# The last stage of a graph kernel: chunks of six buckets summed in PSUM, products on GpSimd, scaled nodes in PSUM

## The chip, the cores and the metric

The kernel runs on one core of one Trainium2 chip. The core has five engines with a queue of instructions each: TensorE (PE in the profile, with its weight loads as PEld), VectorE (DVE), ScalarE (ACT), GpSimd (POOL) and SyncE (SP), which starts transfers here. Each engine works through its queue in order and waits at semaphores for what the others have to deliver. SBUF holds tiles of 128 partitions; PSUM is the memory that TensorE writes its sums to, in 8 banks. The metric is the time of one execution on the device in microseconds, the median of the runs.

## The reference

A graph has N = 6250 nodes with F = 128 features and E = 100,000 edges. The reference runs two graph layers, each followed by a residual and a layer norm. The last stage belongs to the second, cut here to what it computes (`x` is the output of the first layer norm, `edge_attr` has 128 features an edge):

```python
xt = logmap0(x, C)                       # x scaled by one number a node
xs = xt[src]
adj_att = sigmoid(concat([xs, xt[dst], edge_attr]) @ att_w.T + att_b)
agg_add  = segment_sum(xs * adj_att, src, N)
mean_src = segment_sum(edge_attr, src, N) / cnt_src      # cnt = max(edges of the node, 1)
mean_dst = segment_sum(edge_attr, dst, N) / cnt_dst
support_t = xt + agg_add + mean_src + mean_dst
x = layernorm(x + proj(expmap0(support_t, C), C))
```

Since `xs` is summed by its own node, `agg_add` is the node's row times its sum of attentions. `expmap0`, `proj` and the last layer norm need, for each node, the sums of the means, of their squares and of their products with `x`, and then scale whole rows by numbers of the node.

## The kernel before

The kernel sorts edges into 49 *buckets* of 128 source nodes each. Rows of 132 numbers (128 edge features, a one for the count, the attention, and the node's place in its bucket) are scattered by GpSimd's indirect transfers (`scatter`, L812) into tables in memory. The tables of later edges are `lates`; the one of the last edges has 256 rows a bucket, that is two blocks of 128. A bucket is summed by matmuls: `bucket_load` (L1556) fetches its rows into one of four slots of `acc[:, 2]`, `bucket_hot` (L1573) has DVE compare the places with the columns, which makes a one-hot matrix (`oh`, two buffers), and `bucket_mm` (L1587) multiplies it with the rows, so that PSUM holds the features' sums, the count and the attention's sum of 128 nodes (S = 130 columns). `bucket_add` (L1601) adds that to `sums_` in SBUF. In the profile each float32 matmul stands as two passes.

All that runs in a long loop over groups of edges (L1699 to 1718), in an order written out by hand. The *last stage* begins when the last group is scattered: it sums the last table and finishes the nodes. Its order isn't written by hand; a scheduler places its instructions on the engines from their dependencies.

- `chunk(b0)` (L1742) works on CB = 7 buckets. It loads, sums and adds them in two units of four and three. It takes the counts' reciprocals `rc`, and for each bucket DVE adds the mean to `sup` (`mean_dst` so far) and takes its sum `ts` (L1752), and ACT takes the squares' sum `tt` (L1756). DVE multiplies `sup` with the nodes `x1` (L1758) and reduces the products to `tx` (L1759).
- `finish(b0, b1)` (L1761) makes, from `ts`, `tt`, `tx` and the attentions' factor `f`, the three numbers `h`, `m` and `fac` of each node. It is a chain of some 26 short DVE instructions with three ACT functions between (square root L1779, hyperbolic tangent L1781, square root L1796), each change of which loads a table. Then, bucket by bucket, ACT scales the nodes in place (L1805) and DVE adds the scaled `sup` (L1806); SP stores chunks (L1810), and the last part of a bucket by itself (L1818).

Four chunks are followed by `finish(0, 28)`, three by `finish(28, 49)`. PSUM holds the columns' numbers (`beside`, L673), three buffers `bp` of two buckets' sums, and a small check `pq` (L1726).

Of the kernel before, what the change touches and what calls it, by code (L numbers as in the profile page):

```python
# [16 lines left out]
P = 128  # L17
# [585 lines left out]
def window_path(ctx, tc, bad, x, src, dst, edge_attr, edge_weight, Wm1, bm1, Wm2, bm2, Wm3, bm3,  # L603
# [98 lines left out]
    def column(b, name):  # L702
        t = const.tile([F, 1], F32, name=name)
        later(t, b[:, None])
        return t
# [842 lines left out]
        return todo  # L1548
    todo = plan()

    with tc.tile_pool(name="bwork", bufs=2, reuse_waits="tile") as bwork, \
            tc.tile_pool(name="bp", bufs=3, reuse_waits="tile", space=PSUM) as bp:

        n_load = 0

        def bucket_load(us):  # L1556

            nonlocal n_load
            at = n_load % 4 * BR * RW
            n_load += 1  # L1560
            bts = []
            for i, h0, nh in us:
                t, cap = AT[i]
                c = cap // P
                bt = acc[:, 2, at:at + nh * c * RW].rearrange("p (h c f) -> p h c f", h=nh, f=RW)
                at += nh * c * RW
                nc.sync.dma_start(
                    bt.rearrange("p h c f -> p h (c f)"),
                    t[h0 * cap:(h0 + nh) * cap].rearrange("(h p c) f -> p h (c f)", p=P, c=c))
                bts.append(bt)  # L1570
            return bts
# [15 lines left out]
        def bucket_mm(us, bts, ohs):  # L1587
            pbs = []
            for (i, h0, nh), bt, oh in zip(us, bts, ohs):
                c = bt.shape[2]  # L1590
                for a in range(0, nh, 2):
                    pb = bp.tile([P, 2, S], F32, name="pb")
                    n = min(2, nh - a)
                    for h in range(n):
                        for j in range(c):
                            nc.tensor.matmul(pb[:, h], lhsT=oh[:, a + h, j], rhs=bt[:, a + h, j, :S],  # L1596
                                             start=j == 0 and h == 0, stop=j == c - 1 and h == n - 1)
                    pbs.append((i, h0 + a, n, pb))
            return pbs

        def bucket_add(pbs):  # L1601
            for i, h0, n, pb in pbs:
                t = sums_[:, h0:h0 + n]
                if i == 0:
                    nc.scalar.copy(t, pb[:, :n])
                else:
                    nc.vector.tensor_add(t, t, pb[:, :n])

        with tc.tile_pool(name="awork", bufs=2, reuse_waits="tile") as awork, \
                tc.tile_pool(name="ap1", bufs=3, reuse_waits="tile", space=PSUM) as ap1, \  # L1610
                tc.tile_pool(name="ap2", bufs=1, reuse_waits="tile", space=PSUM) as ap2, \
                tc.manual_schedule():
# [110 lines left out]
        with tc.tile_pool(name="fwork", bufs=2, reuse_waits="tile") as fwork, \  # L1723
                tc.tile_pool(name="fp", bufs=1, reuse_waits="tile", space=PSUM) as fp:

            pq = fp.tile([1, P], F32, name="pq")  # L1726
            nc.tensor.matmul(pq, lhsT=badc, rhs=ident, start=True, stop=True)
            nc.vector.tensor_reduce(bad, pq, AX.X, OP.max)

            CB = 7
            assert NB % CB == 0
            last = len(GENS)

            def wide(name):
                return fwork.tile([P, NB], F32, name=name, bufs=1)
            ts, tt, tx, q1, f1 = (wide(n) for n in ("ts", "tt", "tx", "q1", "f1"))
            nc.vector.tensor_mul(q1, mv[:, :, 1], rstd)
            nc.vector.scalar_tensor_tensor(q1, q1, float(F), rstd, op0=OP.mult, op1=OP.mult)  # L1740

            def chunk(b0):  # L1742
                sl = slice(b0, b0 + CB)
                for u in ((last, b0, 4), (last, b0 + 4, 3)):
                    bts = bucket_load([u])
                    bucket_add(bucket_mm([u], bts, bucket_hot([u], bts)))
                s7 = sums_[:, sl]
                rc = fwork.tile([P, CB], F32, name="rc2")
                nc.vector.tensor_scalar(rc, s7[:, :, F], 1.0, None, op0=OP.max)
                nc.vector.reciprocal(rc, rc)  # L1750
                for b in range(CB):
                    nc.vector.scalar_tensor_tensor(sup[:, b0 + b], s7[:, b, :F], rc[:, b:b + 1],  # L1752
                                                   sup[:, b0 + b], op0=OP.mult, op1=OP.add,
                                                   accum_out=ts[:, b0 + b:b0 + b + 1])
                    sq = fwork.tile([P, F], F32, name="sq2")
                    nc.scalar.activation(sq, sup[:, b0 + b], AF.Square, accum_out=tt[:, b0 + b:b0 + b + 1])  # L1756
                xp = fwork.tile([P, CB, F], F32, name="xp")
                nc.vector.tensor_mul(xp, sup[:, sl], x1[:, sl])  # L1758
                nc.vector.tensor_reduce(tx[:, sl], xp, AX.X, OP.add)  # L1759

            def finish(b0, b1):  # L1761
                sl = slice(b0, b1)

                def small(name):
                    return fwork.tile([P, NB], F32, name=name)[:, :b1 - b0]
                h, n2, nrm, un, fac, xn_, m, va = (small(n) for n in (
                    "h", "n2", "nrm", "un", "fac", "xn", "m", "va"))
                f, q = f1[:, sl], q1[:, sl]
                V = nc.vector
                V.scalar_tensor_tensor(f, sums_[:, sl, F + 1], 1.0, att_sum[:, sl], op0=OP.add, op1=OP.add)  # L1770
                V.tensor_mul(f, f, s_log[:, sl])

                V.tensor_mul(h, f, q)
                V.tensor_add(h, h, tx[:, sl])
                V.tensor_add(n2, h, tx[:, sl])
                V.tensor_mul(n2, n2, f)
                V.tensor_add(n2, n2, tt[:, sl])
                V.tensor_scalar(n2, n2, 0.0, None, op0=OP.max)
                nc.scalar.activation(nrm, n2, AF.Sqrt)  # L1779
                V.tensor_scalar(un, nrm, MIN_NORM, None, op0=OP.max)  # L1780
                nc.scalar.activation(fac, un, AF.Tanh)  # L1781
                V.reciprocal(un, un)
                V.tensor_mul(fac, fac, un)
                V.tensor_mul(xn_, fac, nrm)
                V.tensor_scalar(xn_, xn_, MAXNORM, None, op0=OP.max)
                V.reciprocal(xn_, xn_)
                V.scalar_tensor_tensor(fac, xn_, MAXNORM, fac, op0=OP.mult, op1=OP.mult)

                V.scalar_tensor_tensor(m, ts[:, sl], 1.0 / F, fac, op0=OP.mult, op1=OP.mult)
                V.tensor_mul(va, fac, n2)  # L1790
                V.scalar_tensor_tensor(va, h, 2.0, va, op0=OP.mult, op1=OP.add)
                V.tensor_mul(va, va, fac)
                V.tensor_add(va, va, q)
                V.tensor_mul(n2, m, m)
# [6 lines left out]
                V.scalar_tensor_tensor(m, m, -1.0, va, op0=OP.mult, op1=OP.mult)  # L1801
                V.tensor_mul(fac, fac, va)
                for b in range(b0, b1):
                    c = slice(b - b0, b - b0 + 1)
                    nc.scalar.activation(x1[:, b], x1[:, b], AF.Identity, bias=m[:, c], scale=h[:, c])  # L1805
                    V.scalar_tensor_tensor(x1[:, b], sup[:, b], fac[:, c], x1[:, b],  # L1806
                                           op0=OP.mult, op1=OP.add)
                for c0 in range(b0, b1, CB):
                    full = min(c0 + CB, NFULL)
                    nc.sync.dma_start(out[c0 * P:full * P].rearrange("(b p) f -> p b f", p=P), x1[:, c0:full])  # L1810

            for b0 in range(0, 4 * CB, CB):
                chunk(b0)
            finish(0, 4 * CB)
            for b0 in range(4 * CB, NB, CB):
                chunk(b0)
            finish(4 * CB, NB)
            nc.sync.dma_start(out[NFULL * P:], x1[:NREM, NFULL])  # L1818


# [29 lines left out]
```

## Time and profile before

| | |
|---|---|
| median of 3 runs | 2189.34 us (2189.02 to 2191.48) |
| profiled execution, its own time | 2187.51 us |
| its span | 2185.6 us |
| DVE busy over the span | 1637.3 us (75%) |
| PE, ACT, POOL busy over the span | 77%, 42%, 71% |
| mean TensorE clock granted | 0.85 |
| last instruction of the loop on DVE | 2083.5 us |
| last scatter issued on POOL | 2089.65 us |
| four loads of the last table issued on SP | 2092.29 to 2094.29 us |
| first one-hots of the last stage on DVE | 2098.78 us |
| last addition L1806 ends | 2179.07 us |

The last stage is 102 us of the 2185.6. The profile's windows give the busy time of each engine in a stretch, with the number of instructions in brackets, the clock granted to TensorE as a share of full speed, the busy share of the 16 transfer engines and what they moved. Its groups give instructions by line, engine, operation and tile: busy time and mean nanoseconds of one, then the idle time of the engine just before them, and what ended most of it. Its timeline lists start, duration and what an engine waited for. An instruction's recorded duration reaches past the start of the next one on its engine, so the distance from start to start is what it costs its engine in a row.

### The profile page before, as it was taken

The page shows a single profiled execution, that of the slowest core. Times are in us where ns is not written, and L with a number is a line of the kernel's source. Part 1 is how long each engine was busy: PE and PEld are TensorE (multiplying, and loading weights), DVE is VectorE, ACT ScalarE, POOL GpSimd, SP SyncE. Part 2 cuts the span into 40 slices and gives each one's busy share as a digit, 9 for nine tenths or more (in the row PEclk, how much of TensorE's full clock was granted, in tenths as well). Part 3 has the DMA queues.
Part 4 walks back from the last instruction along what each step waited for, and adds up shares of the span by engine and source line. Part 5 has one row for each costly group of instructions (what it writes and reads, how often), then busy time and mean ns, then how long its engine had stood idle before and what let it go on. Part 6 is the DMA issues. An engine that isn't in the chain of part 4 may idle for free. (4 is left out here: it accounts for less than half of the span.)

```text
span 2185.6 us, 41598 instructions
## 1 busy us (share of the span) xinstructions
PE 1674.5 (77%) x13317; PEld 1471.6 (67%) x13317; DVE 1637.3 (75%) x4255; ACT 920.9 (42%) x1580; POOL 1547.0 (71%) x1598
## 2 busy tenths in 40 slices
PE   6778798888778778788878898857777877787642
PEld 5667787777767677677767764446777767677642
DVE  7668888788778788777787854577666876867768
ACT  3755666656556565656555621222111100000016
POOL 3747777777777777777777767777777777777710
PEclk9889898999889899999999977868767987967876
DMA  7777666665666665555454545468888987988832
GB/s 211 199 186 192 173 176 170 169 167 157 177 163 157 166 173 137 137 138 139 134 138 136 137 113 158 121 210 270 255 262 282 305 276 245 314 259 284 271 120 78
DMA packets 344163, 412.75 MB, mean 189 GB/s; under 512 B 53109, under 2 KB 260347, under 8 KB 343681
## 3 DMA queue, kind: packets, MB, share of 16 engines
q1 hardware_dynamic: 292584, 303.65, 48.9%
q0 software_dynamic: 50624, 105.02, 16.4%
q8 instruction: 108, 1.77, 0.3%
q10 hardware_dynamic: 728, 1.33, 0.2%
q14 instruction: 119, 0.97, 0.1%
HBM read 319.79 MB, written 90.00 MB: 187 GB/s over the span
## 5 line engine op out<-in xcount | busy, mean ns | idle before, releaser
L1080 POOL DMA_INDIRECT ga<-p_src,src_i x782 | 751.0, 960 | 270.0 <-issue 208.2
L1596 PE MATMUL pb<-acc,oh 128*128 128x130 f32 x1960 | 326.7, 337 | 64.2 <-DVE oh L1580 34.5
L814 POOL DMA_INDIRECT late<-attr,to_i x298 | 300.8, 1009 | 94.0 <-issue 75.6
L1596 PEld LDWEIGHTS pb<-acc,oh 128*128 128x128 f32 x1960 | 306.9, 246 | 71.6 <-issue 68.2
L1214 PE MATMUL ps<-hot,h 128*128 128x64 f32 x1564 | 296.4, 272 | 0.0
L1188 ACT ACTIVATE h<-pa,bm1c 128x512 f32<-128x512 f32 x196 | 134.5, 686 | 359.2 <-PE pa L1185 358.1
L1230 DVE TENSOR_TENSOR acc<-acc,ps 128x192 f32 x391 | 137.8, 353 | 179.6 <-PE ps L1218 114.1
L1182 PE MATMUL pa<-ident,ga 128*128 128x128 f32 x782 | 162.7, 303 | 138.6 <-DMA ga<-p_src,src_i 128.6
L1199 PEld LDWEIGHTS pb<-wm,h 128*128 128x128 f32 x1564 | 233.5, 214 | 39.4 <-issue 11.9
L1214 PEld LDWEIGHTS ps<-hot,h 128*128 128x128 f32 x1564 | 243.0, 196 | 0.0
L1185 PE MATMUL pa<-feat,lw 128*128 128x256 f32 x782 | 240.6, 438 | 1.4 <-ACT feat L1110 1.4
L1199 PE MATMUL pb<-wm,h 128*128 128x128 f32 x1564 | 230.2, 295 | 1.3 <-ACT h L1188 1.3
L1182 PEld LDWEIGHTS pa<-ident,ga 128*128 128x128 f32 x782 | 100.0, 149 | 170.9 <-DMA ga<-p_src,src_i 168.1
L814 POOL DMA_INDIRECT early<-attr_row,to_i x166 | 166.9, 1005 | 67.2 <-issue 35.0
L1654 PE MATMUL pg<-a,ohT 128*128 128x49 bf16 x2346 | 104.5, 192 | 115.9 <-DVE ohT L1640 115.1
L1216 PE MATMUL ps<-hot,attr 128*128 128x64 f32 x976 | 189.9, 277 | 0.0
L1654 PEld LDWEIGHTS <-ohT 128*128 128x128 bf16 x2346 | 95.8, 101 | 133.9 <-DVE ohT L1640 133.1
L1580 DVE TENSOR_TENSOR oh<-beside,acc 128x896 f32<-128x896 f32 (+3 forms) x149 | 150.7, 1028 | 40.5 <-DMA acc<-late 37.9
L1185 PEld LDWEIGHTS pa<-feat,lw 128*128 128x128 f32 x782 | 157.5, 223 | 17.5 <-ACT feat L1110 1.8
L1640 DVE TENSOR_SCALAR ohT<-los,part 128x2048 bf16<-128x2048 bf16 x98 | 74.8, 764 | 124.6 <-DMA los<-row_lo 124.2
L1666 ACT ACTIVATE attr<-lg,attb 128x5 f32<-128x5 f32 (+1 forms) x60 | 18.2, 304 | 338.2 <-DMA late<-attr,to_i 161.3
L1201 ACT ACTIVATE h<-pb 128x512 f32<-128x512 f32 x196 | 116.4, 594 | 83.6 <-PE pb L1199 78.2
(331 smaller groups left out, 3778.1 us busy)
## 6 DMA issues: line engine op xcount, KB each, us to landing
los<-row_lo SPq DMA_DIRECT2D x98, 512.0 KB
near<-in_edge_weight_dram SPq DMA_DIRECT2D x97, 256.0 KB
attr<-in_edge_attr_dram SPq DMA_DIRECT2D x97, 256.0 KB
acc<-late SPq DMA_DIRECT2D x44, 528.0 KB
acc<-early SPq DMA_DIRECT2D x49, 462.0 KB
late<-zrow SPq DMA_DIRECT2D x22, 792.0 KB
attr<-in_edge_attr_dram SPq DMA_DIRECT2D x256, 64.0 KB
attr<-in_edge_attr_dram SPq DMA_DIRECT2D x118, 128.0 KB
```

Of the source, the lines that this page charges most:

```text
L814: nc.gpsimd.indirect_dma_start(out=t, out_offset=bass.IndirectOffsetOnAxis(ap=to_i[:, b, g:g + 1], axis=0), in_=rows_, in_offset=None)
L1080: nc.gpsimd.indirect_dma_start(out=gas[g][:, b], out_offset=None, in_=p_src[:, :], in_offset=bass.IndirectOffsetOnAxis(ap=src_i[:, b, g:g ...
L1182: nc.tensor.matmul(pa[:, j], lhsT=gas[g][:, 2 * k0 + j], rhs=ident, is_transpose=True, start=j == 0, stop=False)
L1185: nc.tensor.matmul(pa[:, 2 * k:2 * k + 2], lhsT=lws[(4 * g + k0 + k) % NL], rhs=feats[g][:, k0 + k], start=False, stop=k == kk - 1)
L1188: nc.scalar.activation(hid1[i][:, :2 * kk], pa[:, :2 * kk], AF.Silu, bias=bm1c)
L1199: nc.tensor.matmul(pb[:, j], lhsT=h1[:, j], rhs=wm2, start=False, stop=j == nb - 1)
L1214: nc.tensor.matmul(ps[:, k, 0], lhsT=h2[:, 2 * k + c], rhs=hot[:, b], start=k == 0 and c == 0, stop=False)
L1216: nc.tensor.matmul(ps[:, k, 1], lhsT=head[:, b, :F] if b < 3 else rest[:, b - 3], rhs=hot[:, b], start=False, stop=False)
L1230: nc.vector.tensor_add(acc[:, :, bass.ds(at, W)], acc[:, :, bass.ds(at, W)], ps[:, k])
L1580: nc.vector.tensor_tensor(oh.rearrange("p h c e -> p (h c) e"), cols_p[:, None, :].to_broadcast([P, nh * c, P]), bt.rearrange("p h c f -> ...
L1596: nc.tensor.matmul(pb[:, h], lhsT=oh[:, a + h, j], rhs=bt[:, a + h, j, :S], start=j == 0 and h == 0, stop=j == c - 1 and h == n - 1)
L1654: nc.tensor.matmul(pg[:, b, :NB], lhsT=ohT[:, 0, b], rhs=a3[q], start=q == 0, stop=q == 2)
```

## The change

The last stage is cut into chunks of CB = 12 / 2 = 6 buckets, each one unit: one load, one set of one-hots of 12 blocks, and matmuls of six buckets into one tile `pc` of two PSUM banks, three buckets a bank. One addition, written back into PSUM, adds the chunk's part of `sums_` to it, and counts, sums and attentions are read from there. The factor's first sum moves from `finish` into `chunk`, a chunk at a time. The products of `sup` and `x1` are made by GpSimd; their reduction stays on VectorE. In `finish`, ACT writes the scaled nodes to PSUM tiles of the same three buffers `pc`, instead of in place, and VectorE adds from there into `x1`; stores are issued chunk by chunk. There are eight chunks of six and one of one bucket; five chunks are followed by `finish(0, 30)`, four by `finish(30, 49)`. The buffers `bp` end with the loop, which frees their banks.

```diff
-    with tc.tile_pool(name="bwork", bufs=2, reuse_waits="tile") as bwork, \
-            tc.tile_pool(name="bp", bufs=3, reuse_waits="tile", space=PSUM) as bp:
+    with tc.tile_pool(name="bwork", bufs=2, reuse_waits="tile") as bwork:
...
         with tc.tile_pool(name="awork", bufs=2, reuse_waits="tile") as awork, \
+                tc.tile_pool(name="bp", bufs=3, reuse_waits="tile", space=PSUM) as bp, \
...
-            CB = 7
-            assert NB % CB == 0
+            CB = BR // (GENS[-1][1] // P)
...
             def chunk(b0):
-                sl = slice(b0, b0 + CB)
-                for u in ((last, b0, 4), (last, b0 + 4, 3)):
-                    bts = bucket_load([u])
-                    bucket_add(bucket_mm([u], bts, bucket_hot([u], bts)))
-                s7 = sums_[:, sl]
-                rc = fwork.tile([P, CB], F32, name="rc2")
-                nc.vector.tensor_scalar(rc, s7[:, :, F], 1.0, None, op0=OP.max)
+                nb = min(CB, NB - b0)
+                sl = slice(b0, b0 + nb)
+                bts = bucket_load([(last, b0, nb)])
+                oh, = bucket_hot([(last, b0, nb)], bts)
+
+                n = min(3, nb)
+                pc = fp.tile([P, CB // 3, 512], F32, name="pc", bufs=3)
+                sums7 = pc[:, :(nb + 2) // 3, :n * S]
+                for h in range(nb):
+                    c = bts[0].shape[2]
+                    for j in range(c):
+                        nc.tensor.matmul(pc[:, h // 3, h % 3 * S:h % 3 * S + S], lhsT=oh[:, h, j],
+                                         rhs=bts[0][:, h, j, :S], start=j == 0 and h % 3 == 0,
+                                         stop=j == c - 1 and (h % 3 == 2 or h == nb - 1))
+                nc.vector.tensor_add(sums7, sums7, sums_[:, sl].rearrange("p (a b) f -> p a (b f)", b=n))
...
+                rc = fwork.tile([P, CB], F32, name="rc2")[:, :nb]
+                nc.vector.tensor_scalar(of_buckets(rc), column(F), 1.0, None, op0=OP.max)
                 nc.vector.reciprocal(rc, rc)
-                for b in range(CB):
-                    nc.vector.scalar_tensor_tensor(sup[:, b0 + b], s7[:, b, :F], rc[:, b:b + 1],
-                                                   sup[:, b0 + b], op0=OP.mult, op1=OP.add,
+                nc.vector.scalar_tensor_tensor(of_buckets(f1[:, sl]), column(F + 1), 1.0,
+                                               of_buckets(att_sum[:, sl]), op0=OP.add, op1=OP.add)
+                for b in range(nb):
+                    nc.vector.scalar_tensor_tensor(sup[:, b0 + b], pc[:, b // 3, b % 3 * S:b % 3 * S + F],
+                                                   rc[:, b:b + 1], sup[:, b0 + b], op0=OP.mult, op1=OP.add,
                                                    accum_out=ts[:, b0 + b:b0 + b + 1])
...
-                nc.vector.tensor_mul(xp, sup[:, sl], x1[:, sl])
-                nc.vector.tensor_reduce(tx[:, sl], xp, AX.X, OP.add)
+                nc.gpsimd.tensor_tensor(xp[:, :nb], sup[:, sl], x1[:, sl], op=OP.mult)
+                nc.vector.tensor_reduce(tx[:, sl], xp[:, :nb], AX.X, OP.add)
...
-                V.scalar_tensor_tensor(f, sums_[:, sl, F + 1], 1.0, att_sum[:, sl], op0=OP.add, op1=OP.add)
                 V.tensor_mul(f, f, s_log[:, sl])
...
-                for b in range(b0, b1):
-                    c = slice(b - b0, b - b0 + 1)
-                    nc.scalar.activation(x1[:, b], x1[:, b], AF.Identity, bias=m[:, c], scale=h[:, c])
-                    V.scalar_tensor_tensor(x1[:, b], sup[:, b], fac[:, c], x1[:, b],
-                                           op0=OP.mult, op1=OP.add)
                 for c0 in range(b0, b1, CB):
-                    full = min(c0 + CB, NFULL)
-                    nc.sync.dma_start(out[c0 * P:full * P].rearrange("(b p) f -> p b f", p=P), x1[:, c0:full])
-
-            for b0 in range(0, 4 * CB, CB):
+                    c1 = min(c0 + CB, b1)
+                    px = fp.tile([P, CB // 3, 512], F32, name="pc", bufs=3)
+                    for b in range(c0, c1):
+                        c = slice(b - b0, b - b0 + 1)
+                        at = (b - c0) * F
+                        y = px[:, at // 512, at % 512:at % 512 + F]
+                        nc.scalar.activation(y, x1[:, b], AF.Identity, bias=m[:, c], scale=h[:, c])
+                        V.scalar_tensor_tensor(x1[:, b], sup[:, b], fac[:, c], y, op0=OP.mult, op1=OP.add)
+                    full = min(c1, NFULL)
+                    if full > c0:
+                        nc.sync.dma_start(out[c0 * P:full * P].rearrange("(b p) f -> p b f", p=P),
+                                          x1[:, c0:full])
+
+            H = 5 * CB
+            for b0 in range(0, H, CB):
                 chunk(b0)
-            finish(0, 4 * CB)
-            for b0 in range(4 * CB, NB, CB):
+            finish(0, H)
+            for b0 in range(H, NB, CB):
                 chunk(b0)
-            finish(4 * CB, NB)
+            finish(H, NB)
```

More of the change, by code (lines that the diff above doesn't have):

```diff
@@ new lines, in chunk, with column, of_buckets @@
+                nc.vector.tensor_add(sums7, sums7, sums_[:, sl].rearrange("p (a b) f -> p a (b f)", b=n))
+                def column(k):
+                    return sums7.rearrange("p a (b f) -> p a b f", f=S)[:, :, :, k]
+                def of_buckets(t):
+                    return t.rearrange("p (a b) -> p a b", b=n)
+                rc = fwork.tile([P, CB], F32, name="rc2")[:, :nb]
+                nc.vector.tensor_scalar(of_buckets(rc), column(F), 1.0, None, op0=OP.max)
+                nc.vector.reciprocal(rc, rc)
```

## The prediction

> **What bounds the kernel now.** Only the last stage changes: the order of the instructions before it is the same in both kernels, so everything up to 2083.5 us of the span is taken as unchanged. I read the stage first by windows (each engine's busy time in each stretch), then by groups, then in order of time. The windows:
>
> ```profile
> core 0: us, PE busy (x) PEld busy (x) DVE busy (x) ACT busy (x) POOL busy (x), PEclk, DMA share, GB/s
> 2083.50:2098.80 15.30, 0.00 (x0) 0.00 (x0) 0.04 (x2) 0.00 (x0) 5.59 (x6) 0.58 0.46 152
> 2098.80:2106.50 7.70, 6.03 (x39) 5.90 (x40) 5.40 (x9) 0.00 (x0) 0.00 (x0) 0.72 0.26 65
> 2106.50:2151.30 44.80, 24.97 (x160) 23.80 (x158) 44.33 (x169) 17.96 (x90) 0.00 (x0) 0.85 0.34 97
> 2151.30:2163.40 12.10, 0.00 (x0) 0.00 (x0) 12.07 (x50) 12.09 (x37) 0.00 (x0) 0.62 0.39 115
> 2163.40:2171.00 7.60, 0.00 (x0) 0.00 (x0) 4.55 (x27) 4.66 (x13) 0.00 (x0) 0.50 0.20 61
> 2171.00:2179.10 8.10, 0.00 (x0) 0.00 (x0) 7.38 (x21) 7.68 (x20) 0.00 (x0) 0.50 0.40 115
> 2179.10:2185.60 6.50, 0.00 (x0) 0.00 (x0) 0.00 (x0) 0.00 (x0) 0.00 (x0) 0.50 0.28 74
> ```
>
> The first row is the wait for the last scatters and loads. In the next three DVE is the bound: 44.33 of 44.80 us busy, while POOL does nothing. The chunks and the first `finish` are interleaved there, so the short instructions and table loads of that `finish` lie beside the chunks' work. The row of 7.60 us is the second `finish` alone: a chain of short dependent steps, DVE busy a little over half of it. The row of 8.10 us is 21 nodes' scaling and addition, and the last is the output's way to memory. What DVE's time consists of, and who paces the end, from the groups of this stage:
>
> ```profile
> L1805 ACT ACTIVATE x<-x,m,h 128x128 f32<-128x128 f32 x49 | 19.1, 481 | 1.7 <-DVE m L1801 1.7
> ...
> L1752 DVE SCALAR_TENSOR_TENSOR acc<-acc,rc 128x128 f32<-128x128 f32 x49 | 14.8, 349 | 0.0
> ...
> L1607 DVE TENSOR_TENSOR acc<-acc,pb 128x260 f32<-128x260 f32 x21 | 8.9, 423 | 2.8 <-PE pb L1596 2.8
> L1580 DVE TENSOR_TENSOR oh<-beside,acc 128x1024 f32<-128x1024 f32 x7 | 8.6, 1222 | 15.3 <-DMA acc<-late 15.3
> L1758 DVE TENSOR_TENSOR xp<-acc,x 128x896 f32<-128x896 f32 x7 | 7.6, 1088 | 0.0
> L1759 DVE TENSOR_REDUCE tx<-xp 128x7 f32<-128x896 f32 x7 | 7.5, 1069 | 0.0
> ```
>
> These durations overlap at their ends, so sums are made with the distance from start to start. The timeline of the end shows how that is read, and the two paces of the last row:
>
> ```profile
> 2161.42 1.09 DVE L1759 TENSOR_REDUCE tx<-xp 128x7 f32<-128x896 f32 x1
> 2162.42 1.14 DVE L1806 SCALAR_TENSOR_TENSOR x<-acc,fac,x 128x128 f32<-128x128 f32 x4
> ...
> 2166.84 0.29 DVE L1782 RECIPROCAL un<-un 128x21 f32<-128x21 f32 x1 [1.35 <-ACT fac L1781]
> ...
> 2171.03 8.04 DVE L1806 SCALAR_TENSOR_TENSOR x<-acc,fac,x 128x128 f32<-128x128 f32 x21 [0.47 <-ACT x L1805]
> ```
>
> The reduction of 896 elements lasts 1.09 but the next starts after 1.00. Four additions that wait for nobody take 1.14 (0.265 a step); the last 21 take 8.04 (0.386), since ACT scales them at that pace. So a node costs 0.265 where DVE is the bound and 0.386 where it waits for ACT.
>
> **The change, part by part.** Steps on DVE, from such distances: one-hots 1.13 for 1024 elements and 0.86 for 768, which makes 1.66 for 1536 (0.06 and 1.05 ns an element, from (1.13 - 0.86) over 256); addition of two buckets 0.34, so 0.88 for 780 elements; the mean's addition L1752 0.272; reduction 0.87 for 768.
>
> *DVE's list.* One-hots fall from 7 x 1.99 = 13.9 us to 13.6; additions from 7 x 1.22 = 8.5 to 8 x 0.88 + 0.2 = 7.2; the products leave (7 x 1.0 = 7.0); the reductions stay at 7.1; reciprocals and the factor's sum, now once a chunk, grow from 1.4 to 2.7. The 49 mean additions (13.3), 49 last additions (13.0) and the two sets of short steps (5.4) stay. Sum: 69.6 before, 62.3 after, a gain of **7.3 us** if DVE has as few gaps as now. It now spans 80.3 us (2098.8 to 2179.1), so it has 10.7 us of gaps.
>
> One rule speaks against reading these operands from PSUM. The Trainium skill (Perfetto Trace Analysis, Optimizing Scalar/DVE Operations) gives some 60 ns of overhead a DVE instruction on SBUF and 125 on PSUM; by it the 49 mean additions would cost 49 x 0.065 = 3.2 us more. The trace doesn't agree: L1607, which reads PSUM, has 0.34 - 260 x 0.00105 = 0.07 of overhead, as L1758 has, which doesn't; and L1128 writes PSUM in 0.30 us for 147 elements, beside 0.31 for L1130 into SBUF. I take nothing, and keep 3.2 for the range.
>
> *Products on POOL.* It is idle, so its own time is free; but the reduction on DVE waits for it, and all behind it on DVE waits too. No row shows arithmetic on POOL; the nearest is the same product on DVE, 0.87 us for 768. The skill (GPSIMD Engine Reference, Elementwise — side-by-side cycle accounting) has a two-input operation at 1.96 times DVE's, 4497 ns for 2048 elements, which makes an estimate of 1.7 us here. I take 1.75; ends 0.9 and 2.2. In the changed order the reduction stands behind other DVE work for chunks 0 to 3 (gaps about 0.8 us in all), but nearly bare for chunk 4, before the first `finish` (1.5), and thinly covered for chunks 5 to 8 (0.9 to 1.2 each, 3.3 in all). Gaps: **5.6 us**.
>
> *First `finish`.* In the changed order its 27 short steps stand in one row on DVE, with no chunk's work between. The chain that the window of 7.60 us shows has 2.7 us of steps; so some 4.7 us of gaps appear that were covered before. Its third table load also waits for the variance here, which it doesn't now; a table load has 1283 ns in the groups: 1.3 more. Gaps: **6.0 us**.
>
> *Scaled nodes in PSUM.* All 30 nodes of that `finish` are then added in one row, at ACT's pace instead of DVE's. ACT also has to wait, from the fourth on, until DVE has read the node before it in the same PSUM tile: a round of 0.53 (ACT start to DVE start, 2170.50 to 2171.03) + 0.35 + 0.05 = 0.93 us, spread over three tiles for 18 nodes (0.31, hidden under 0.386) and over two for 12 (0.47). Gaps: 18 x 0.12 + 12 x 0.2 = **4.6 us**. Whether ACT is quicker into PSUM no row shows. From PSUM it is by about 0.04 (L1605's 254 ns for 130 elements beside L1756's 297 for 128); bounds 0 to 0.1 a node; I take 0.025, which gives 49 x 0.025 = 1.2 us back.
>
> *PE and buffers.* The matmuls stay 196 passes. The sums of chunk 5 need the PSUM tile that node 18 frees; 24 passes in the slow clock (0.18 each in 2101 to 2103, where the windows show 11 in 2 us) take 4.3 us and end about when the 30 nodes do: 0.2. The first addition waits for 24 passes rather than 4, DVE having the second one-hots meanwhile: 2.6, beside 2.8 now.
>
> *Second `finish`.* Its chain keeps its gaps (4.7). 19 nodes at ACT's pace: 19 x 0.12 = 2.3, beside 2.5 for 21 now.
>
> *Loads.* Four loads leave SP together:
>
> ```profile
> 2092.29 2.00 SPq L1567 DMA_DIRECT2D acc<-late  x4
> ```
>
> The first one-hots use the third of them now and the second afterwards, 1.62 MB instead of 1.45 in front of them at some 340 GB/s: 0.4 us later. Later loads are four slots ahead and stay hidden.
>
> *Output.* Nodes of three chunks are now finished in turn, so the last three stores, 1.18 MB, leave together behind the last additions, where now one of 0.39 MB does. At the 270 to 290 GB/s of the stores that adds some **2.2 us** of the 2.7 at full rate.
>
> *Sum.* DVE from first one-hots to last addition: 62.3 + 2.6 + 5.6 + 6.0 + 4.6 + 0.2 + 4.7 + 2.3 = 88.3, less 1.2 = 87.1 us, beside 80.3. With 0.4 for the load and 2.2 for the output: +9.4. Such sums of gaps count some overlaps twice; I take **+8.5 us**. The span becomes 2194, the profiled execution 2196 (1.9 us lie around the span, as in 2187.51 beside 2185.6). The median of the runs shown is 1.8 above that execution: **2197.8 us**.
>
> **Rivals.**
> 1. *Forecast, +4.4 to +13:* the gain of DVE goes into waits for POOL, ACT and the table loads. Chance 0.60.
> 2. *About even:* POOL multiplies at DVE's own pace (0.9) and ACT's step into PSUM falls by 0.1. The gaps for POOL shrink from 5.6 to about 1.4, ACT's by up to 4.9 in all, instead of 1.2: 8.5 - 4.2 - 3.7 = +0.6, 2190 us. For it: POOL is idle and has no other work; against it: the only price known. Chance 0.20.
> 3. *Faster:* DVE's shorter list decides, as it does in the row of 44.80 us. This needs the first `finish` to leave DVE busy. From a product under 1 us and an ACT step under 0.28 on, and with the output's last stores hidden as well, 7.3 gained beside some 4 of new gaps: 2183 to 2186. Against it: the chain of 7.60 us stands bare twice. Chance 0.07.
> 4. *Much slower:* POOL takes over 2.5 us, or its first product pays a load of its code (about 6 us in the same page, Instruction dispatch; no run here shows it). Each microsecond of product costs some 7: 2204 or more. Chance 0.13.
> That the arithmetic isn't moved is no rival; the changed order shows it on POOL.
>
> **Numbers.** 0.2% is 4.4 us, about what can be told from no change. Faster: rival 3, 0.07; within: rival 2, 0.20; slower: 0.73. Range: from rival 2's middle, 2190, to the low end of rival 4, 2204; it leaves out some 0.07 at either side besides half of the even case.
>
> **What would show it.** DVE's waits should name POOL (some 5 us), and ACT twice in a row of short steps; a product on POOL of 1.7 us; the 30 additions in about 12.7 us; no chunk work on DVE for some 20 us after chunk 4. Wrong would be: products under 1 us, additions at 0.27 a step, or a last addition before 2179 us.

## The result, and the profile after

| | before | changed |
|---|---|---|
| median of 6 runs each, side by side | 2189.38 us (2187.77 to 2191.63) | 2206.26 us (2202.06 to 2210.84) |
| profiled execution / its span | 2187.51 / 2185.6 us | 2205.41 / 2203.6 us |
| last scatter issued on POOL | 2089.65 us | 2092.20 us |
| from there to the first one-hots | 9.13 us | 9.77 us |
| first one-hots to the last addition's end | 80.29 us | 91.90 us |
| behind the last addition | 6.53 us | 9.73 us |

The changed kernel takes 1.0077 of the time before (95% interval 1.0062 to 1.0092): 16.9 us more, where 8.5 were forecast. The last three rows add up to 95.95 and 111.40, so the last stage is 15.45 us longer in these two profiles; the other 2.55 lie ahead of it. The changed kernel's last stage by windows, cut where DVE's work changes (start and end of a window, its length, then each engine's busy time with its count):

```profile
core 0: us, PE busy (x) PEld busy (x) DVE busy (x) ACT busy (x) POOL busy (x), PEclk, DMA share, GB/s
...
2101.97:2109.40 7.43, 5.57 (x26) 5.60 (x27) 3.42 (x2) 0.00 (x0) 0.00 (x0) 0.50 0.54 176
2109.40:2140.21 30.81, 13.78 (x96) 13.42 (x95) 27.47 (x93) 10.60 (x61) 9.08 (x5) 0.78 0.36 110
2140.21:2149.01 8.80, 0.00 (x0) 0.00 (x0) 4.42 (x24) 3.83 (x7) 0.00 (x0) 0.50 0.00 1
2149.01:2161.34 12.33, 5.35 (x26) 5.38 (x27) 10.09 (x29) 11.49 (x29) 0.00 (x0) 0.52 0.34 97
2161.34:2179.36 18.02, 6.80 (x52) 6.14 (x50) 15.77 (x62) 6.10 (x38) 5.87 (x4) 0.77 0.16 46
2179.36:2186.61 7.25, 0.00 (x0) 0.00 (x0) 4.18 (x27) 3.81 (x7) 0.00 (x0) 0.50 0.01 2
2186.61:2193.87 7.26, 0.00 (x0) 0.00 (x0) 6.60 (x19) 6.88 (x18) 0.00 (x0) 0.50 0.03 9
2193.87:2203.60 9.73, 0.00 (x0) 0.00 (x0) 0.00 (x0) 0.00 (x0) 0.00 (x0) 0.50 0.44 126
```

The rows of 8.80 and 7.25 us are the two chains of `finish`: before, only one stood alone. In the first of them VectorE, the busiest engine, works for half of the time. The row of 12.33 is 29 additions of the first `finish` in one line, at ACT's pace; the last row is the output, with the transfer engines busy 0.44 of it rather than 0.28. Chunk 5 (the sixth) stood ready long before that: DVE made its one-hots from 2128.11 us on, but PE began to sum it at 2155.99, 0.1 behind the addition of the 18th of the 30 nodes. By the program that is when its tile of the ring comes free:

```profile
2128.11 1.75 DVE L1579 TENSOR_TENSOR oh<-beside,acc 128x1536 f32<-128x1536 f32 x1
...
2155.99 7.99 PE L1753 MATMUL pc<-acc,oh 128*128 128x130 f32 x48 [26.30 <-issue]
```

The bracket is PE's idle time, for which the profile names no engine ("issue"). What DVE waited for (us in all, times, longest), from the changed kernel's waits:

```profile
engine line waited for: us in total, times, longest us
DVE oh L1579 <- DMA acc<-late: 16.7, 1, 16.7
DVE tx L1776 <- POOL xp L1775: 5.4, 5, 1.7
DVE pc L1756 <- PE pc L1753: 4.7, 2, 4.0
DVE un L1798 <- ACT fac L1797: 2.7, 2, 1.4
DVE va L1813 <- ACT va L1812: 2.1, 2, 1.7
DVE x L1827 <- ACT pc L1826: 1.0, 2, 0.5
DVE un L1796 <- ACT nrm L1795: 0.6, 2, 0.3
```

POOL is named with 5.4 us, and each wait for ACT's functions comes twice. The groups that answer to those shown of before:

```profile
L1826 ACT ACTIVATE pc<-x,m,h 128x128 f32<-128x128 f32 x49 | 19.4, 444 | 1.7 <-DVE fac L1818 1.5
```

```profile
L1579 DVE TENSOR_TENSOR oh<-beside,acc 128x1536 f32<-128x1536 f32 (+1 forms) x9 | 14.2, 1588 | 16.7 <-DMA acc<-late 16.7
...
L1769 DVE SCALAR_TENSOR_TENSOR acc<-pc,rc,acc 128x128 f32<-128x128 f32 x49 | 14.0, 347 | 0.0
L1756 DVE TENSOR_TENSOR pc<-pc,acc 128x780 f32<-128x780 f32 (+1 forms) x9 | 8.0, 893 | 4.7 <-PE pc L1753 4.7
...
L1776 DVE TENSOR_REDUCE tx<-xp 128x6 f32<-128x768 f32 (+1 forms) x9 | 7.8, 877 | 5.5 <-POOL xp L1775 5.4
...
L1787 DVE TENSOR_TENSOR f<-f,s_log 128x30 f32<-128x30 f32 (+1 forms) x2 | 1.6, 824 | 0.0
```

Reading PSUM costs the mean's addition nothing: 347 ns beside 349. ACT is 37 ns quicker into PSUM (444 beside 481). The last line is odd: a multiplication of 30 elements a partition, with a mean of 824 ns. The timeline of all engines shows the slow one of the two:

```profile
2176.28 1.80 POOL L1775 TENSOR_TENSOR xp<-acc,x 128x768 f32<-128x768 f32 x1 [2.48 <-DVE acc L1769]
...
2176.38 0.16 DVE L1764 TENSOR_SCALAR rc<-pc 128x1 f32<-128x1 f32 x1
2176.46 0.15 DVE L1766 SCALAR_TENSOR_TENSOR f<-pc,att_sum 128x1 f32<-128x1 f32 x1
...
2176.57 0.16 DVE L1765 RECIPROCAL rc<-rc 128x1 f32<-128x1 f32 x1
2176.65 1.46 DVE L1787 TENSOR_TENSOR f<-f,s_log 128x19 f32<-128x19 f32 x1
2178.03 0.34 DVE L1769 SCALAR_TENSOR_TENSOR acc<-pc,rc,acc 128x128 f32<-128x128 f32 x1
...
2178.30 1.14 DVE L1776 TENSOR_REDUCE tx<-xp 128x6 f32<-128x768 f32 x2
```

It lasts 1.46 us where the other takes 0.19, and ends with POOL's product (2178.08). Steps of DVE that read one operand from PSUM run on beside POOL, and so does the reciprocal, which has one operand; this one, with both operands in SBUF, stands still. Its bracket is empty, so no list of waits shows it: 1.3 us lost to POOL beside the 5.4. They are not a cost of their own, though. The last line shown is the reduction of that same product; had L1787 not been held, DVE would have waited there instead, and by an estimate from these times the reduction would have started only some 0.2 us sooner.

### The profile page after: what moved, and what is told of

Same layout as the page of the kernel before. It is cut to its first block, busy times and chain, and to the rows that moved or that the text cites. A ratio compares the mean times of both kernels' runs of the same rounds, so it can differ in the third digit from the quotient of the medians.

```text
span 2203.6 us, 41592 instructions
## 1 busy us (share of the span) xinstructions
PE 1684.7 (76%) x13317; PEld 1481.4 (67%) x13317; DVE 1638.0 (74%) x4237; ACT 922.1 (42%) x1580; POOL 1563.7 (71%) x1607
## 5 line engine op out<-in xcount | busy, mean ns | idle before, releaser
L1080 POOL DMA_INDIRECT ga<-p_src,src_i x782 | 756.1, 967 | 264.6 <-issue 213.9
L1595 PE MATMUL pb<-acc,oh 128*128 128x130 f32 x1764 | 299.9, 341 | 30.1 <-DVE oh L1579 16.0
L1595 PEld LDWEIGHTS pb<-acc,oh 128*128 128x128 f32 x1764 | 281.3, 250 | 36.7 <-issue 32.5
L1199 PEld LDWEIGHTS pb<-wm,h 128*128 128x128 f32 x1564 | 239.4, 219 | 40.2 <-issue 12.8
L1199 PE MATMUL pb<-wm,h 128*128 128x128 f32 x1564 | 235.6, 300 | 1.3 <-ACT h L1188 1.3
L1579 DVE TENSOR_TENSOR oh<-beside,acc 128x896 f32<-128x896 f32 (+4 forms) x144 | 150.0, 1057 | 44.6 <-DMA acc<-late 42.6
L1666 ACT ACTIVATE attr<-lg,attb 128x5 f32<-128x5 f32 (+1 forms) x60 | 18.2, 304 | 342.9 <-DVE lg L1665 163.5
```

What stands on the lines that cost most here:

```text
L1080: nc.gpsimd.indirect_dma_start(out=gas[g][:, b], out_offset=None, in_=p_src[:, :], in_offset=bass.IndirectOffsetOnAxis(ap=src_i[:, b, g:g ...
L1199: nc.tensor.matmul(pb[:, j], lhsT=h1[:, j], rhs=wm2, start=False, stop=j == nb - 1)
L1579: nc.vector.tensor_tensor(oh.rearrange("p h c e -> p (h c) e"), cols_p[:, None, :].to_broadcast([P, nh * c, P]), bt.rearrange("p h c f -> ...
```

## The experiments

**Which part makes the first `finish` bare.** In the changed kernel the scaled nodes take tiles of the ring that holds the chunks' sums, and stand ahead of chunk 5 in the program. Two kernels tell the ring apart from PSUM as a place; in the first, nodes are scaled in place.

```diff
-                    px = fp.tile([P, CB // 3, 512], F32, name="pc", bufs=3)
...
-                        at = (b - c0) * F
-                        y = px[:, at // 512, at % 512:at % 512 + F]
+                        y = x1[:, b]
```

> The changed kernel, but ACT scales the nodes in place in SBUF as before, so the tiles pc hold chunks' sums alone. In the changed kernel a scaled node takes the next tile of the same ring as chunk 5's sums, and stands ahead of it in the program; so the scheduler can't put chunk 5 beside the first finish. Without these tiles the order on VectorE shows chunk 5's to 8's work between the short steps again. My theory (the tile ring makes the first finish bare): the changed kernel's 2206.3 us lose the 6.0 of the bare chain, the 4.6 of additions at ACT's pace, 0.2 and some 2 of the stores, and give back 1.2 of ACT's quicker writes: about 2194.5 us, within 3. Rival (chunks of six, the longer start and GpSimd's products cost it, the ring doesn't): no gain over 3 us, 2203 or more.

Measured: 2188.79 us, 1.0004 of the kernel before (0.9994 to 1.0015). More came back than expected: 2206.3 less 2188.8 is 17.5 us, where 11.8 were forecast. The last stage takes 95.02 us from the last scatter on, 16.4 less than in the changed kernel: 12.9 between first one-hots and last addition, 3.2 behind it, 0.3 ahead. DVE's timeline of this kernel where the first `finish` begins:

```profile
2142.33 0.34 DVE L1769 SCALAR_TENSOR_TENSOR acc<-pc,rc,acc 128x128 f32<-128x128 f32 x1
...
2142.60 0.18 DVE L1792 TENSOR_TENSOR n<-n,f 128x30 f32<-128x30 f32 x1
2142.70 0.34 DVE L1769 SCALAR_TENSOR_TENSOR acc<-pc,rc,acc 128x128 f32<-128x128 f32 x1
...
2142.97 0.18 DVE L1793 TENSOR_TENSOR n<-n,tt 128x30 f32<-128x30 f32 x1
...
2143.91 1.75 DVE L1579 TENSOR_TENSOR oh<-beside,acc 128x1536 f32<-128x1536 f32 x1
2145.71 0.28 DVE L1796 TENSOR_SCALAR un<-nrm 128x30 f32<-128x30 f32 x1
```

Chunk work stands between the chain's steps, and no bracket is left: the square root is covered by one-hots. Its waits show a second effect, which the expectation missed:

```profile
...
DVE pc L1756 <- PE pc L1753: 3.7, 1, 3.7
DVE tx L1776 <- POOL xp L1775: 2.1, 3, 0.8
DVE un L1798 <- ACT fac L1797: 1.4, 1, 1.4
```

Of POOL's 5.4 us of waits 3.3 are gone. But two steps with both operands in SBUF are now held during a product, for 0.9 and 1.6 us, the second of them an in-place addition (one of the three in the last line here, which take 0.3 each elsewhere):

```profile
2152.37 1.09 DVE L1811 SCALAR_TENSOR_TENSOR va<-va,n 128x30 f32<-128x30 f32 x1
...
2157.96 2.44 DVE L1825 SCALAR_TENSOR_TENSOR x<-acc,fac,x 128x128 f32<-128x128 f32 x3
```

Waits and held steps together fall from 6.7 to 4.6 us, so some 2 of the 16.4 us lie here; the others are the bare chain, the additions behind it and the output. In the next kernel POOL takes 7.9, so this part doesn't follow from the ring as such.

The second kernel keeps PSUM, but gives the nodes tiles of their own:

```diff
-                pc = fp.tile([P, CB // 3, 512], F32, name="pc", bufs=3)
+                pc = fp.tile([P, CB // 3, 512], F32, name="pc", bufs=2)
...
+                        if (b - b0) % 4 == 0:
+                            px = fp.tile([P, 4, F], F32, name="px", bufs=2)
...
+                        y = px[:, (b - b0) % 4]
```

> The changed kernel, with the scaled nodes still in PSUM, but in two tiles of their own of one bank (four nodes each), and two buffers for the chunks' sums rather than three. It tells the ring from the place: my theory (the shared ring is what counts) has the first finish beside the chunks again, so the 6.0 us of its chain go and part of the 4.6; but some 26 nodes then stand bare at the end rather than 19, 2.7 more: about 2199 us. Rival (PSUM as the place costs it): as the changed kernel, 2205 or more.

Measured: 2198.84 us (1.0047, 1.0031 to 1.0063). The time is the one expected, but by luck: the last stage takes 100.02 us, 11.4 less than in the changed kernel where 7.3 were expected, and the part ahead of it ended late (last scatter at 2099.98). Behind the last addition it needs 6.59 us. Chunk work stands between the first chain's steps here too:

```profile
2151.42 0.18 DVE L1792 TENSOR_TENSOR n<-n,f 128x30 f32<-128x30 f32 x1
2151.51 0.34 DVE L1769 SCALAR_TENSOR_TENSOR acc<-pc,rc,acc 128x128 f32<-128x128 f32 x1
...
2151.78 0.18 DVE L1793 TENSOR_TENSOR n<-n,tt 128x30 f32<-128x30 f32 x1
```

So the shared ring makes the first `finish` bare, and PSUM as a place doesn't. Of the 5.0 us by which this stage is longer than with scaling in place, 3.3 are POOL's (4.8 of waits, 3.1 of held steps); this kernel also has one tile fewer for the chunks. That chunk 5 placed ahead of the nodes in the ring would do as well was not run.

**The products.**

```diff
-                nc.gpsimd.tensor_tensor(xp[:, :nb], sup[:, sl], x1[:, sl], op=OP.mult)
+                nc.vector.tensor_mul(xp[:, :nb], sup[:, sl], x1[:, sl])
```

In the changed kernel:

> The changed kernel, but the products of nodes and means are made on VectorE. My theory: the waits for GpSimd (5.4 us in its trace) and a two-input step held for 1.3 us while GpSimd multiplies go, and 49 products of 0.14 us, 7.1 in all, come back to VectorE: 2206.7 us, within 2 of the changed kernel. Rival (GpSimd slows VectorE more than the waits show, by their common access to SBUF): 2202 or less.

Measured: 2205.33 us (1.0074, 1.0058 to 1.0089), as my theory had it. The waits for POOL are gone, and L1787 takes 0.17 and 0.19 us. In the changed order, then, the move to GpSimd is worth about nothing: its 5.4 of waits and 1.3 of held step are about the 7.1 that it saves.

In the kernel that scales in place:

> The changed kernel with nodes scaled in place and products on VectorE: of the change only the chunks of six, summed in PSUM, are left. My theory: without the bare chain VectorE is the bound again, so the products' 7.1 us count, less some 3 of waits for GpSimd that go: 2 to 5 us above the kernel that only scales in place, near 2197. Rival (products on GpSimd are the loss): below that kernel by 2 us or more, near 2190.

Measured: 2191.59 us (1.0016, 1.0009 to 1.0024), 2.8 above in-place scaling alone, as the theory had it, though the intervals overlap a little. (It is 5 under the figure of 2197, since in-place scaling came out as much faster than expected.) The last stage is 4.7 longer (99.76), of which 2.4 are waits for PE (6.1 us instead of 3.7). With chunk work to fill the gaps, the move pays some 2.5 us: 7.1 saved for 4.6 of waits and held steps.

In the kernel before, alone, the move was run on two chips. On the first, every kernel, the one before too, took over 2800 us; of the runs there only what lies behind the first one-hots is used here.

```diff
-                nc.vector.tensor_mul(xp, sup[:, sl], x1[:, sl])
+                nc.gpsimd.tensor_tensor(xp, sup[:, sl], x1[:, sl], op=OP.mult)
```

> The kernel before, with only the products moved to GpSimd. My theory: VectorE's list falls by 7.0 us; where chunks lie between product and reduction the wait is small, so waits of some 3.5 us and stalls of some 1 come back: 2185.7 us, within 2. Rival (GpSimd's products are a loss by themselves, about as much as their waits of 5.4 us in the changed kernel): 2191 or more.

> The kernel before with only the products on GpSimd, once more. On the disturbed chip its last stage took 92.3 us from the first one-hots to the end, 5.5 more than the kernel before: waits for GpSimd 5.3, for PE 3.0 more, and VectorE steps with both inputs in SBUF held for some 3. My theory now: the waits and held steps outweigh the 7.0 us saved here, and PE's part shrinks on an undisturbed chip: 2190.5, within 2. Rival (my first figure): 2186 or less.

Measured: 2856.20 beside 2857.20 us (1.0006, 0.9971 to 1.0040), and the second time 2201.59 beside 2192.55 us (1.0045, 1.0029 to 1.0061). My first figure was on the wrong side, and the second, 2190.5, was 11 too low. In the second profile DVE waits 6.0 us for POOL, and steps are held too:

```profile
2150.20 2.08 POOL L1758 TENSOR_TENSOR xp<-acc,x 128x896 f32<-128x896 f32 x1 [6.04 <-DVE acc L1752]
2150.32 0.41 DVE L1607 TENSOR_TENSOR acc<-acc,pb 128x260 f32<-128x260 f32 x1
...
2150.68 1.64 DVE L1780 TENSOR_SCALAR un<-nrm 128x28 f32<-128x28 f32 x1
...
2152.32 1.09 DVE L1759 TENSOR_REDUCE tx<-xp 128x7 f32<-128x896 f32 x1
```

L1607, which reads PSUM, starts and ends inside the product; L1780, from SBUF to SBUF, takes 1.64 us instead of 0.18 and ends with it. An in-place node addition is held likewise (two of L1806 take 2.45 us there, 0.61 elsewhere). Waits of 6.0 and some 3.3 of held steps (1.5 and 1.8) outweigh the 7.0 saved by 2.3, and waits for PE come to 5.2 us (2.8 and 4.2 in the two profiles of the kernel before). Here too most of the held time stands in for a wait: behind L1780 comes the reduction of the same product. Between first one-hots and end this kernel takes 90.73 us, the one before 86.82 and, in its second profile below, 89.00. So 1.7 to 3.9 us of the 9 lie there; the rest lies ahead of the last stage, which neither expectation had.

**PSUM as a place, alone, in the kernel before** (on the chip where every kernel took over 2800 us):

```diff
-                    nc.scalar.activation(x1[:, b], x1[:, b], AF.Identity, bias=m[:, c], scale=h[:, c])
...
+                    if (b - b0) % 4 == 0:
+                        px = fp.tile([P, 4, F], F32, name="px", bufs=3)
+                    y = px[:, (b - b0) % 4]
+                    nc.scalar.activation(y, x1[:, b], AF.Identity, bias=m[:, c], scale=h[:, c])
```

> The kernel before, with only the scaled nodes put into PSUM, in three tiles of their own of one bank (four nodes each), so nothing of the chunks waits for them. My theory (PSUM as a place costs or gives next to nothing; ACT is 37 ns a node quicker, and the last 21 nodes gain by that at most 0.8 us): 2187.8 us, within 1.5. Rival (reading PSUM costs VectorE 65 ns more an instruction): 49 x 0.065 = 3.2 more, 2191.4.

Measured: 2861.34 beside 2857.20 us (1.0014, 0.9983 to 1.0045), which tells nothing at this width. The duration does: DVE's addition from PSUM takes 346 ns, in place 351. The rival's 65 ns aren't there.

**The start.** The chunk of one bucket goes first instead of last:

```diff
...
-            H = 5 * CB
-            for b0 in range(0, H, CB):
+            H = 5 * CB + 1
+            chunk(0, 1)
+            for b0 in range(1, H, CB):
```

> The changed kernel with its chunk of one bucket first instead of last (31 nodes in the first finish, 18 in the second). The first addition then waits for 4 PE passes rather than 24. My theory (the longer start is worth what its wait shows): the wait of 4.0 us for PE shrinks to about 1.5: 2203.8 us, within 1.5. Rival (PE's slow clock at the start only moves the wait to the second addition): 2206, as the changed kernel.

> The changed kernel with its chunk of one bucket first, once more, since the first look fell on a chip where every kernel took 2800 us and more. There, from the first one-hots on, it took 101.5 us as the changed kernel does (101.6): the wait for PE fell by 2.0, but a load was waited for instead and GpSimd more. My theory now: on an undisturbed chip the loads come in time, and it gains 1 to 2.5: 2204 to 2205. Rival (the wait only moves on): 2206.

Measured: 2865.83 beside 2857.20 us (1.0017, 0.9993 to 1.0041), and the second time 2204.90 beside 2192.55 us (1.0067, 1.0054 to 1.0080); the changed kernel has 1.0077, so some 2 us are gained at most, and the intervals overlap. The last stage is 1.7 us shorter (109.71). But the reason is another. The wait for PE only moves to the second addition:

```profile
2102.69 0.29 DVE L1755 TENSOR_TENSOR pc<-pc,acc 128x130 f32<-128x130 f32 x1
...
2108.10 0.98 DVE L1755 TENSOR_TENSOR pc<-pc,acc 128x780 f32<-128x780 f32 x1 [2.67 <-PE pc L1752]
```

With two waits it comes to 4.1 us (4.7 in the changed kernel), and the stretch from the first one-hots on takes 102.0 us (101.6). What is gained lies ahead of that: with a small first load the first one-hots come 7.69 us behind the last scatter, not 9.77. The same edit on the kernel that scales in place:

> The kernel that scales nodes in place (2188.8 us), with the chunk of one bucket first. My theory: its wait of 3.7 us for PE shrinks to about 1.2, so 2186.3 us, within 1.5, and a little below the kernel before. Rival (the wait only moves): 2188.5 or more.

> In-place scaling with the chunk of one bucket first, once more, for the same reason. From the first one-hots to the end it took 85.0 us on the disturbed chip, beside 85.5 for in-place scaling alone and 86.8 for the kernel before. My theory: 0.5 to 2 us below in-place scaling alone, so 2186.8 to 2188.3. Rival (nothing gained): 2188.8 or more.

Measured: 2849.08 beside 2857.20 us (0.9988, 0.9963 to 1.0012), then 2191.76 beside 2192.55 us (0.9994, 0.9985 to 1.0004). Its last stage is the shortest of all, 92.48 us, 3.5 under the kernel before, yet its time can't be told from that kernel's: the last scatter comes at 2098.12.

**The output.** In-place scaling again, with the second half's output stored behind its last addition:

```diff
-                    if full > c0:
+                    if full > c0 and b0 == 0:
...
+            nc.sync.dma_start(out[H * P:NFULL * P].rearrange("(b p) f -> p b f", p=P), x1[:, H:NFULL])
```

> The kernel that scales in place (2188.8 us, 6.5 us from the last addition to the end of its span), with the output of the second finish, 1.18 MB, stored behind its last addition rather than chunk by chunk. My theory (the changed kernel's 9.7 us behind its last addition are stores that leave together): 9.5 to 10.5 us behind the last addition, and 2192.3 us, within 1. Rival (the tail is a fixed latency, the changed kernel's longer one comes of something else): 6.5 to 7 us, and 2189.

Measured: 8.55 us behind the last addition, between theory and rival; 2198.72 beside 2192.55 us (1.0032, 1.0020 to 1.0045), where 2192.3 were expected. The last stage is 2.7 us longer than with in-place scaling alone (97.76); the rest lies ahead of it (last scatter at 2098.14). SP's timeline tells what the 2.0 us more behind the last addition are. First this kernel, then the changed one, then the one that scales in place:

```profile
2187.00 0.37 SPq L1838 DMA_DIRECT2D out_dram<-x  x1
2187.46 2.08 SPq L1839 DMA_DIRECT2D out_dram<-x  x1
```

```profile
2193.21 1.44 SPq L1830 DMA_DIRECT2D out_dram<-x  x2
2194.74 1.17 SPq L1840 DMA_DIRECT2D out_dram<-x  x1
```

```profile
2180.21 2.68 SPq L1828 DMA_DIRECT2D out_dram<-x  x2
2182.98 0.36 SPq L1838 DMA_DIRECT2D out_dram<-x  x1
```

With in-place scaling alone the last store, 106 rows, is issued in 0.36 us and through 0.5 us behind the last addition (2183.34); the span ends 6.1 later. Behind one large store its issue takes 2.08, and is through 2.2 behind the last addition (2189.54); the span ends 6.4 later. In the changed kernel it stands behind others, takes 1.17 and is through 2.0 behind (2195.91); the span ends 7.7 later. So of the changed kernel's 3.2 us, 1.6 pass until the last issue on SP is through, and 1.6 behind it. My theory counted bytes alone, and they don't explain the second part: the kernel with one large store has as many bytes, 1.18 MB, to move there, and only 0.3 more behind its issue. That part stays open.

**The part ahead of the last stage.** Both kernels again, unchanged:

> The kernel before, unchanged, for a second profile. If the part ahead of the last stage only differs from one execution to the next: its last scatter is issued anywhere from 2088 to 2098 us, and the last stage from there to the end takes 96 us within 1.

> The changed kernel, unchanged, for a second profile. The last stage from the last scatter to the end takes 111.4 us within 1, 15.4 more than in the kernel before. If the part ahead of it only differs from one execution to the next, the median is 15.4 us above the other's, within 2, and the last scatter comes at no fixed distance from the other's. Rival (the change makes the earlier part longer by 2.6 us too): 18 us above it.

Measured: 2192.06 us beside 2191.28 (1.0004, 0.9992 to 1.0016) and 2208.16 us (1.0078, 1.0056 to 1.0101). The last scatter was issued at 2089.05 and 2095.58 us, and the last stage took 98.55 and 110.22. The kernel before missed its 96 by 2.6; in this execution it waited 4.2 us for PE rather than 2.8, and 0.4 more for its loads, and 0.8 I can't place; the changed kernel missed its 111.4 by 1.2, half of it in a shorter wait for PE (3.3). So 11.7 us lie in the last stage here, 6.5 ahead of it; the medians differ by 16.1, which is within the theory's 15.4 and 2. In the other profiles on chips of about 2190 us the last scatter comes at 2088.3 to 2100.0 us; the kernel before with products on GpSimd has it at 2099.1. The cause is open: on DVE, ACT, POOL and SP the instructions there are the same and in the same order, and the granted clock up to 2080 us is 0.85 or 0.86 in all these profiles. The traces give a lead. The lag builds up over the whole loop: in the kernel before with products on GpSimd, POOL's instructions come 3.5 us later than in the kernel before at 640 us, 6.9 at 1250 and 9.5 at 1990. And it goes with the place of the products: the four profiles with products on VectorE have the last scatter at 2088.3 to 2093.4, the eight with products on GpSimd at 2092.2 to 2100.0, though the first product runs only behind it. The 782 gathers that POOL issues (L1080) take 959 to 964 ns on average in those four and 966 to 971 in those eight; why, and whether this is the cause, no run shows.

## Why the prediction was right in kind and wrong in size

| its term | forecast | measured |
|---|---|---|
| the part ahead, "taken as unchanged" | 0 | +2.6, +6.5 in a second profile; cause open |
| loads (1.49 MB in front before, not 1.45) | +0.4 | +0.6 |
| wait for PE before the first addition | 2.6 | 4.0 (second profile 3.3) |
| waits for POOL, product on POOL | 5.6, 1.75 | 5.4, 1.81 |
| DVE steps held by POOL | none | 1.3 (with the waits 6.7) |
| first `finish` bare, with its third table load | 6.0 above 2.7 of steps | chain of 8.8 |
| 30 nodes at ACT's pace, less ACT's gain | 12.55 - 0.75 = 11.8 | 29 in 11.66, so 12.05 |
| sums of chunk 5 | 0.2 | 0.7 |
| second chain | 7.4 | 7.25 |
| 19 nodes at ACT's pace, less ACT's gain | 7.35 - 0.45 = 6.9 | 7.26 |
| output | +2.2 | +3.2 |
| "I take" less than the sum | -0.9 | no such overlap |

**Right:** the direction and its mechanism. DVE's shorter list went into waits for POOL, a bare first `finish` and ACT's pace. The chains and the rows of nodes came out within 0.4 us each, what POOL costs 1.1 higher. The kernels without the shared ring show that the bare chain and the additions behind it have one cause: 11.4 us of the stage's length go with tiles of their own, 16.4 with scaling in place. PE's part and most of POOL's remain.

**Wrong:** the size, by 8.4 us (2206.3 beside 2197.8), and the range, which ended at 2204. In the first profile the span grew by 18.0, not 9.4. Of these 8.6 us, 2.55 lie in the part ahead, the step that I took as unchanged. The stage has 6.05: 4.8 between one-hots and last addition (87.1 forecast, 91.9 measured), 1.0 in the output, 0.2 in the load. Of the 4.8, 3.6 have a name: PE's wait (+1.4), POOL's waits and held step (+1.1), the two rows of nodes (+0.6) and chunk 5 (+0.5); the rest is spread over steps too small to assign. In the second pair of profiles the span grew by 18.2, and of the 8.8 above the forecast 6.5 lie in the part ahead and 2.3 in the stage. So the step that failed most, in both pairs, is "everything up to 2083.5 us is taken as unchanged", which put the part ahead at nothing; the others are terms of the stage that were too small, above all PE's wait, POOL and the output.

*PE's wait.* I priced 24 passes at 0.18 us, since the window from 2101 to 2103 of the kernel before counts 11 in 2 us:

```profile
2101.00:2103.00 2.00, 2.00 (x11) 2.00 (x11) 0.43 (x1) 0.00 (x0) 0.00 (x0) 0.50 0.03 8
```

That count was misread: it takes in passes that reach over the window's edges. From start to start a pass takes 0.22 us there, at a granted clock of 0.50, and just as much in the changed kernel at the same clock; 24 of them, from 2103.83 on, last till the addition at 2109.40. At a clock of 1.0 a pass takes 0.11. The wait also depends on when the clock rises: in the kernel before it had 13 passes behind it, in the changed kernel 26, and in its second profile 17, where the wait was 3.3 us.

*ACT.* The gain of 37 ns a node was real and worth nothing. A shorter recorded duration isn't a shorter step: 19 nodes took 7.26 us into PSUM, 7.27 in place in the other kernel. A pace is measured from start to start.

*POOL.* The prediction moved the products onto an idle engine and asked only who waits for it. The Trainium skill (SBUF — State Buffer, SBUF: two separate sides) says that VectorE and GpSimd share a pair of ports under an exclusive lock, and that a VectorE step in a two-port mode, or with two SBUF operands against a GpSimd step that reads SBUF, stands still until the other is through, if that one started first. The traces agree for two SBUF operands: L1787 and L1811 end with the product (1.46 and 1.09 us instead of 0.19), and steps that read PSUM pass. L1780, with one operand, is held too (1.64 us); whether it runs in a two-port mode no trace shows. By that rule held steps should have been a term, but a small one: most of their time DVE would have spent waiting for the same product. What was too small is POOL's term as a whole, 5.6 us where waits and held step make 6.7.

*The allowance.* Taking 8.5 of 9.4 for overlaps had no row behind it.

**Rivals.** "Much slower" named 2204 or more, by a product over 2.5 us or a load of code. That time came, but not so: the product takes 1.81 us, the first 1.80. "About even" and "faster" needed a product of under 1 us and a quicker row of additions; the product took twice that, and the row kept ACT's pace. "Some 7" for a microsecond of product was too much by the prediction's own gaps: 5.6 less 1.4 for 0.85 us makes 5.

## What to carry to other kernels

Before giving a tile of an existing ring to a later stage, look at what the ring's next user in the program is: it can no longer be scheduled ahead of that stage, and the stage's short dependent steps then stand alone. When work goes to GpSimd, ask what VectorE does in the meantime: enough of it to cover the product, and with operands that aren't all in SBUF. A saved microsecond on the busiest engine counts only where the order leaves that engine something else to do.

## What the hardware showed beside that

A held DVE step carries no wait in the profile: it is just long (1.46 and 1.64 us for steps of 0.18), so it is found by comparing durations within one line, and the second profile of the changed kernel repeats it (1.46). What it costs is read from the next step that needs the other engine's result. And since the part ahead of the last stage, with the same instructions, ended anywhere between 2088 and 2100 us, differences of a few microseconds in a span of 2190 are read from the stage, not from the total.
